# Three more turns through DRAM blocks, four bias additions on GpSimd, the inner hat on ScalarE and key loads of half the size

## The chip, the core and the metric

The kernel runs on one core of a Trainium2 chip. The metric is the device time of one execution in microseconds. The kernel before took 3769.52 us, the median of three runs (3765.85 to 3770.04).

The core's engines run side by side, each through its own list of instructions in order: TensorE (PE in the profile, its weight loads PEld), VectorE (DVE), ScalarE (ACT), GpSimd (POOL) and SyncE (SP), which here only issues transfers. An instruction that waits for another engine or a transfer holds up all that stand behind it on its own engine.

## What is computed

Input `x` is four images of 64 x 64 pixels with 256 channels, in float32. First comes full self-attention within each image, then a deformable convolution (DCNv3) and an MLP. Cut to what matters:

```python
q, k, v = x @ wq + bq, x @ wk + bk, x @ wv + bv          # per image, 4096 pixels
x = gamma * (softmax(q @ k.T) @ v) + x

h = ln(x, ln1_g, ln1_b)
x_proj = h @ inproj_w + inproj_b
x1 = depthwise_conv_3x3(h, dw_w) + dw_b
x1 = gelu(ln(x1, dwln_g, dwln_b))
offset = x1 @ off_w + off_b                               # 16 groups x 9 points x (x, y)
mask = softmax(x1 @ mask_w + mask_b)                      # over the 9 points
out = sum over points of mask * bilinear(x_proj, point + offset)
x = x + out @ outproj_w + outproj_b
h = ln(x, ln2_g, ln2_b)
x = x + gelu(h @ fc1_w + fc1_b) @ fc2_w + fc2_b
```

## The kernel before, in words

**Tiling.** 256 pixels (4 image rows) are a unit; there are 64 units, 16 an image. A unit goes through these stages, each a Python function that returns named steps:

- `project` (from line 1391): load the unit's pixels, turn them so that channels lie on partitions, make keys, queries and values. `value_bias` (line 1453) adds the value bias on VectorE while it moves the values out of PSUM. For the first image the values go straight to the tiles `V`, for the others to DRAM (`vd`), from where `value_load` brings them.
- `Attention` (line 1474): works on two units of queries at once. Keys come from DRAM in four loads `k0` to `k3` of 512 KB into two buffers, issued on SP. Step `e<j>` multiplies keys by queries (PE, line 1544), `x<j>` takes exponentials (ACT, line 1554), `wa<j>` and `wb<j>` multiply them with the values (PE, line 1565). `own` loads the pixels for the residual.
- `front` (line 1585): `inverse` and `residual` divide by the softmax sum and add the residual, `stats`, `shift` and `norm` make the first layer norm, `turn` transposes its result on PE (four 128 x 128 transposes through `transposed`, line 347), `scale` applies gain and bias, `image` copies into the convolution's input `hs`, `project_in` is `inproj_w` and `store` adds its bias and sends it to DRAM (`xp`). `keep` adds the output projection's bias to the residual and sends that to DRAM (`x1d`).
- `plan` (line 1644): nine taps of the depthwise convolution on VectorE into `cv` (line 1670), `turn` back to pixels on partitions (PE, line 1683), a layer norm, `turn2` (PE, line 347), `gelu`, the offset and mask heads, and then the bilinear weights as products of three hats an axis: `hat0` and `hat2` are relu(-d) and relu(d) on ScalarE (line 1734), `hat1` is 1 - hat0 - hat2 on VectorE (line 1738).
- `sample` (line 1869): loads windows of `xp` (`win`), and multiplies and adds them with the weights on VectorE (lines 1880 and 1888, 1280 elements a partition each).
- `back`, by `finish` (line 1948): output projection, residual, layer norm, MLP. `raised` (line 1989) adds the last bias on VectorE.

**Turning through DRAM blocks.** VectorE's transpose instruction turns 32 x 32 blocks inside a tile and does not move blocks between partitions. So the kernel has a second way to turn: the tile is written to DRAM (`ways`), read back by four transfers that put the 32 x 32 blocks in their mirrored places (`in_blocks`, line 70, through `blocks`, line 285), and one VectorE instruction then turns all blocks (`swapped`, line 290). Before, this serves `project` of the images after the first (directly from the input) and the two turns of `back` (line 1955 and 1991) for all but the first pair of row groups and the last six. A turn on PE needs no transfer.

**Statistics.** Each layer norm has two small GpSimd instructions on 128 x 2 elements (lines 304 and 305) between VectorE's `stats` and `shift`. Apart from a few setup instructions that is all that GpSimd computes.

**Order.** The order on PE, VectorE, ScalarE and GpSimd is written out by hand in tables: `WHEN` (line 355) gives each step of each stage a place in a slot of nominally 120, and `LATE` holds other places for the first and last slots. Steps of about six stages of different units are so interleaved in each slot. The places are only sorted; they are no times. A slot holds two units.

The kernel also contains a general version of the whole pass for inputs whose values leave a safe range. It is in the program, but isn't executed with these inputs.

Of the kernel before, what the change touches and what calls it, by code (L numbers as in the profile page):

```python
# [8 lines left out]
F32 = mybir.dt.float32  # L9
# [11 lines left out]
def tile_attention_dcnv3_block(  # L21
# [26 lines left out]
    P = 128  # L48
# [234 lines left out]
    ways = dram.tile([2, 256, C], F32, name="ways")  # L283

    def blocks(name, src, t0=0):
        t = p1.tile([P, C // P, 256], F32, tag="xs", name=f"bl_{name}")
        in_blocks(t, src, t0, 2)
        return t

# [32 lines left out]
    def scaled(pt, g, b, name, m=256, hT=None):  # L322

        if hT is None:
            hT = p3.tile([P, C // P, 256], F32, tag="cT", name=f"hT_{name}")
# [16 lines left out]
    def transposed(src, name, n=2, pool=None, tag="m"):  # L342

        pt = (pool or ps).tile([P, C // P, 256], F32, tag=tag, name=f"pt_{name}")
        for k in range(C // P):
            for i in range(n):
# [11 lines left out]
            "value_bias": 7.4,  # L358
# [3 lines left out]
            "value_bias": 7.4,  # L362
        },
        "projecta": {
            "load": 0.5607, "copy": 16.2617, "turn": 19.72, "keys": 32.3364, "key_bias": 36.8224,
            "values": 63.7383, "value_bias": 68.2243,
        },
        "projectb": {
            "load": 65.9813, "turn": 79.72, "copy": 80.9346, "keys": 136.6355, "key_bias": 137.757,
            "values": 167.6636, "value_bias": 171.4019,  # L370
        },
        "tablesa": {
            "gelu0": -44.2991, "gelu1": -13.6449, "exp": -12.8972,
        },
        "tablesb": {
            "gelu0": -9.1589, "gelu1": 54.0187, "exp": 61.1215,
        },
        "fronta": {
            "inverse": -7.6636, "residual": -6.9159, "stats": -6.1682, "shift": -3.5514, "norm": 19.2523,
            "turn": 22.243, "scale": 24.486, "image": 24.8598, "project_in": 25.9813, "store": 33.4579,  # L380
            "keep": 40.1869,
        },
        "frontb": {
            "inverse": 4.2991, "residual": 10.6542, "stats": 20.0, "shift": 49.5327, "norm": 52.1495,
            "turn": 60.3738, "scale": 65.6075, "image": 66.3551, "keep": 71.215, "project_in": 78.3178,
            "store": 84.6729,
        },
        "plana": {
            "tap0": 25.6075, "tap1": 26.729, "tap2": 28.5981, "tap3": 30.4673, "tap4": 31.215, "tap5": 32.7103,
            "tap6": 34.2056, "tap7": 34.5794, "tap8": 38.6916, "turn": 40.9346, "stats": 45.0467,  # L390
            "shift": 48.0374, "norm": 49.1589, "turn2": 51.028, "gelu": 51.7757, "heads0": 54.7664,
            "heads1": 55.514, "bias0": 57.0093, "bias1": 61.8692, "mask_exp": 62.243, "sums": 62.9907,
            "carry": 63.3645, "invert": 64.8598, "weigh": 66.729, "hat0": 69.7196, "hat2": 70.8411,
            "hat1": 75.3271, "nearer": 78.6916, "near": 79.0654, "mask": 81.3084, "product0": 81.6822,
            "y_copies0": 83.1776, "y0": 83.5514, "product1": 84.2991, "y1": 85.7944, "y_copies1": 88.0374,
            "x_copies": 88.785, "x": 92.8972, "count": 111.5888, "bounds": 246.9159,
        },
        "planb": {
            "tap0": 69.3458, "tap1": 73.8318, "tap2": 80.5607, "tap3": 86.1682, "tap4": 89.1589,
            "tap5": 89.9065, "tap6": 91.028, "tap7": 93.6449, "tap8": 94.7664, "turn": 96.6355,  # L400
            "carry": 98.5047, "stats": 99.6262, "shift": 102.6168, "norm": 104.8598, "turn2": 107.8505,
            "gelu": 108.5981, "heads0": 113.4579, "heads1": 114.5794, "bias0": 116.0748, "bias1": 116.8224,
            "hat0": 117.9439, "mask_exp": 118.6916, "sums": 119.4393, "hat2": 122.4299, "hat1": 122.8037,
# [104 lines left out]
    }  # L508


    LATE = {
        "summinga": {
            32: {
                "rows01": -68.11728, "rows02": -65.41895, "rows03": -60.32211, "rows04": -52.22712,
# [1842 lines left out]
```

## Time and profile before

| what | value | where it is from |
|---|---|---|
| median of 3 runs | 3769.52 us (3765.85 to 3770.04) | times |
| profiled execution | 3769.71 us | times |
| its span, first to last instruction | 3767.9 us | profile |
| PE busy, weight loads (PEld) busy | 3674.0 us (98%), 3089.0 us (82%) | profile, part 1 |
| DVE busy | 3494.9 us (93%) | profile, part 1 |
| ACT busy | 2286.7 us (61%) | profile, part 1 |
| POOL busy | 464.4 us (12%) | profile, part 1 |
| granted TensorE clock | 0.993 mean | profile, cores |
| transfers | 507.21 MB, 135 GB/s mean | profile, part 3 |

The span is the time from the first to the last instruction that the profiler saw. Engine shares are of that span. In groups of instructions (part 5 of the profile) a line reads: source line, engine, operation, written tile <- read tiles, shape, count, then busy time in us, mean ns of one, and the idle time of the engine just before them with what ended it. In the timeline a row reads: start in us, duration in us, engine, line, operation.

### The profile page before, as it was taken

The page shows a single profiled execution, that of the slowest core. Times are in us where ns is not written, and L with a number is a line of the kernel's source. Part 1 is how long each engine was busy: PE and PEld are TensorE (multiplying, and loading weights), DVE is VectorE, ACT ScalarE, POOL GpSimd, SP SyncE. Part 2 cuts the span into 40 slices and gives each one's busy share as a digit, 9 for nine tenths or more (in the row PEclk, how much of TensorE's full clock was granted, in tenths as well). Part 3 has the DMA queues.
Part 4 walks back from the last instruction along what each step waited for, and adds up shares of the span by engine and source line. Part 5 has one row for each costly group of instructions (what it writes and reads, how often), then busy time and mean ns, then how long its engine had stood idle before and what let it go on. Part 6 is the DMA issues. An engine that isn't in the chain of part 4 may idle for free.

```text
span 3767.9 us, 49959 instructions
## 1 busy us (share of the span) xinstructions
PE 3674.0 (98%) x16770; PEld 3089.0 (82%) x16770; DVE 3494.9 (93%) x6107; ACT 2286.7 (61%) x4164; POOL 464.4 (12%) x444
## 2 busy tenths in 40 slices
PE   7999999999999999999999999999999999999978
PEld 5888888888888888888888888888888888887757
DVE  2289999999999999999999999999999999999996
ACT  2465666665666665666665666665666666666633
POOL 1001011101111101111101101101101110110021
PEclk9999999999999999999999999999999999999989
DMA  6354455555555454546555545545645444444331
GB/s 170 105 150 130 132 140 137 138 149 155 135 152 147 134 133 131 142 129 173 145 137 147 144 126 139 139 131 153 160 121 150 130 121 114 129 132 133 109 90 53
DMA packets 609404, 507.21 MB, mean 135 GB/s; under 512 B 380816, under 2 KB 538576, under 8 KB 609136
## 3 DMA queue, kind: packets, MB, share of 16 engines
q1 hardware_dynamic: 599232, 497.00, 49.6%
q10 hardware_dynamic: 8320, 3.43, 0.4%
q0 software_dynamic: 1584, 3.47, 0.3%
q8 instruction: 135, 2.21, 0.3%
q14 instruction: 133, 1.09, 0.1%
HBM read 351.31 MB, written 152.44 MB: 134 GB/s over the span
## 4 chain that ended last, share of the span: by engine, by line
DVE 62%; PE 18%; issue 7%; DMA 4%; POOL 4%; ACT 3%; SPq 1%; DVEq 0%; ACTq 0%; POOLq 0%
DVE pw L1888 14%; DVE pw L1880 13%; DVE cv L1670 8%; PE acc L1565 8%; DVE pr L1793 3%; PE pmlp L2024 2%; PE ph L2007 2%; POOL rstd_b L305 2%; DVE pw L1893 1%; DVE om L1716 1%; DVE hat L1785 1%; PE e L1544 1%; POOL rstd_b L304 1%; DVE st_b L300 1%; DVE x L1595 1%
## 5 line engine op out<-in xcount | busy, mean ns | idle before, releaser
L1565 PE MATMUL acc<-V,ex 128*128 128x257 f32 x8192 | 1888.2, 380 | 1.3 <-ACT ex L1554 1.2
L1565 PEld LDWEIGHTS acc<-V,ex 128*128 128x128 f32 x8192 | 1546.7, 190 | 239.8 <-issue 20.7
L1880 DVE TENSOR_TENSOR pw<-win,wn 128x1280 f32<-128x1280 f32 x640 | 944.7, 1482 | 10.7 <-DMA win<-xp 1.7
L1888 DVE TENSOR_TENSOR pw<-pw,pw 128x1280 f32<-128x1280 f32 x492 | 727.8, 1479 | 0.4
L1554 ACT ACTIVATE ex<-e 128x512 f32<-128x512 f32 x1024 | 553.3, 590 | 260.0 <-PE e L1544 229.9
L2007 PE MATMUL ph<-hT_b,f1w 128*128 128x256 f32 (+1 forms) x2080 | 509.0, 382 | 23.3 <-ACT gT L2015 13.6
L2007 PEld LDWEIGHTS ph<-hT_b,f1w 128*128 128x128 f32 x2080 | 386.9, 192 | 100.1 <-ACT gT L2015 30.0
L2024 PE MATMUL pmlp<-f2w,gT 128*128 128x256 f32 x2048 | 463.2, 380 | 0.3 <-ACT gT L2015 0.3
L1670 DVE SCALAR_TENSOR_TENSOR cv<-hs,dw,cv 128x256 f32<-128x256 f32 (+1 forms) x1076 | 433.9, 462 | 3.9 <-ACT cv L1666 3.8
L2024 PEld LDWEIGHTS pmlp<-f2w,gT 128*128 128x128 f32 x2048 | 386.3, 191 | 53.4 <-ACT gT L2015 0.7
L1544 PE MATMUL e<-qs,kT 128*128 128x512 f32 (+1 forms) x1056 | 418.3, 479 | 10.1 <-issue 6.2
L2015 ACT ACTIVATE gT<-ph,f1b 128x256 f32<-128x256 f32 (+1 forms) x520 | 237.7, 468 | 191.9 <-PE ph L2007 189.6
L1554 ACT ACT_TABLE_LOAD x220 | 282.3, 1283 | 8.3 <-PE acc L1565 4.8
L304 POOL TENSOR_SCALAR rstd_b<-mv_b 128x2 f32<-128x2 f32 (+1 forms) x65 | 59.8, 920 | 1658.4 <-DVE mv_b L302 1596.6
L1544 PEld LDWEIGHTS e<-qs,kT 128*128 128x128 f32 x1056 | 196.3, 191 | 42.8 <-ACT ex L1554 9.3
L318 ACT ACTIVATE xn_b<-x1b,nm_b,rstd_b 128x256 f32<-128x256 f32 x128 | 70.0, 593 | 238.1 <-DVE nm_b L310 237.3
L1707 PE MATMUL po<-om_w,ge 128*128 128x432 f32 x512 | 201.7, 535 | 4.4 <-ACT ge L1700 3.6
L1793 DVE TENSOR_TENSOR pr<-hat 128x1296 f32<-128x1296 f32 x128 | 192.6, 1505 | 5.8 <-ACT us L1808 1.8
L318 ACT ACTIVATE xn_p<-pc,nm_p,rstd_p 128x256 f32<-128x256 f32 x128 | 65.3, 559 | 218.0 <-DVE nm_p L310 218.0
L2015 ACT ACT_TABLE_LOAD x136 | 174.5, 1283 | 2.4
L1707 PEld LDWEIGHTS po<-om_w,ge 128*128 128x128 f32 x512 | 98.0, 193 | 74.9 <-issue 51.7
L304 POOL TENSOR_SCALAR rstd_f<-mv_f 128x2 f32<-128x2 f32 x64 | 25.1, 393 | 1078.9 <-DVE mv_f L302 1029.3
(224 smaller groups left out, 4042.8 us busy)
## 6 DMA issues: line engine op xcount, KB each, us to landing
win<-xp SPq DMA_DIRECT2D x536, 320.0 KB, 4.4
kT<-kd SPq DMA_DIRECT2D x132, 512.0 KB, 3.9
omd<-om SPq DMA_DIRECT2D x63, 432.0 KB, 2.5
x<-in_x_dram SPq DMA_DIRECT2D x64, 256.0 KB, 3.2
x1d<-x SPq DMA_DIRECT2D x64, 256.0 KB, 2.8
xp<-xq SPq DMA_DIRECT2D x128, 128.0 KB, 2.4
x1b<-x1d SPq DMA_DIRECT2D x63, 256.0 KB, 3.0
spd<-sp SPq DMA_DIRECT2D x63, 256.0 KB, 2.2
```

The costliest lines, as they stand in the source:

```text
L318: nc.scalar.activation(xn[:, i, :], s, AF.Identity, bias=nm[:, i : i + 1], scale=st["r"][:, i : i + 1])
L1544: nc.tensor.matmul(e, lhsT=self.kT[t // 8][:, t % 8, :], rhs=q, start=True, stop=not self.general)
L1554: nc.scalar.activation(ex, self.es[r], AF.Exp)
L1565: nc.tensor.matmul(self.acc[u][:, i, :], lhsT=ex[:, i * P : (i + 1) * P], rhs=V[j][:, jj, :], start=(t == 0), stop=(t == NT - 1),)
L1670: nc.vector.scalar_tensor_tensor(dst, src, dw[:, k, j : j + 1], dst, ALU.mult, ALU.add)
L1707: nc.tensor.matmul(st["po", i], lhsT=st["ge"][:, k, i * P : (i + 1) * P], rhs=om_w[:, k, :], start=(k == 0), stop=(k == 1),)
L1793: nc.vector.tensor_mul(pr.rearrange("p a b c d g -> p a b (c d g)"), hat[:, :, i, 1, :].unsqueeze(1).to_broadcast([P, 3, 3, S]), hat[:, :, ...
L1880: nc.vector.tensor_mul(st[i, r].rearrange("p d (g c) -> p (d g) c", c=GC), src.rearrange("p d (g c) -> p (d g) c", c=GC), wns[v][:, i, r] ...
L1888: nc.vector.tensor_add(st[i, 0], st[i, 0], st[i, r])
L2007: nc.tensor.matmul(ph[:, :m], lhsT=f1w[:, k, c * P : (c + 1) * P], rhs=st["hT"][:, k, :m], start=(k == 0), stop=(k == 1),)
L2015: nc.scalar.activation(st["gT"][:, c, :m], st["ph", c][:, :m], AF.Gelu, bias=f1b[:, c : c + 1])
L2024: nc.tensor.matmul(po, lhsT=st["gT"][:, c, i * P : (i + 1) * P], rhs=f2w[:, c, :], start=(c == 0), stop=(c == NH - 1),)
```

## The change

Five things are changed, and both order tables are written anew.

1. **Turns.** `front.turn` (layer-normed image), `plan.turn` (convolution) and `plan.turn2` (its normalised form) go through DRAM blocks like the turns of `back`: `sent` writes the tile to one of eight buffers `ways`, `blocks` reads it, `swapped` turns it on VectorE. This holds for units 0 to 57 in `front` and pairs 1 to 57 in `plan`; the rest keep PE. For `back` the range shrinks from pairs 1 to 58 to pairs 1 to 55. Writes of normalised tiles are issued on ScalarE's queue, that of the convolution on SP.
2. **Bias additions.** `keep`, `store` (now a ScalarE copy out of PSUM, then a new step `add`), `raised` and the value bias become GpSimd additions of 128 x 512 elements. The value bias is no longer added to the values: since softmax weights sum to one it is added once to the residual's pixels (new steps `biasa`, `biasb`), and values leave PSUM by a ScalarE copy (`value_copy`).
3. **Inner hat.** `hat1` becomes two ScalarE instructions: |d|, then 1 - |d|.
4. **Keys.** Eight loads of 256 KB instead of four of 512 KB, still into two buffers (each half as large), issued on ScalarE's queue instead of SP's.
5. **Buffers.** `cT` gets four buffers instead of three, `xs` two instead of one.

```diff
-    ways = dram.tile([2, 256, C], F32, name="ways")
+    ways = dram.tile([8, 256, C], F32, name="ways")

     def blocks(name, src, t0=0):
-        t = p1.tile([P, C // P, 256], F32, tag="xs", name=f"bl_{name}")
+        t = p1.tile([P, C // P, 256], F32, tag="xs", bufs=2, name=f"bl_{name}")
         in_blocks(t, src, t0, 2)
         return t
+
+    def sent(k, u, src, engine):
+        way = ways[2 * k + u % 2]
+        engine.dma_start(way.rearrange("(q p) c -> p q c", p=P), src)
+        return way
...
-        def value_bias():
-            bias = bv_s.unsqueeze(1).to_broadcast([P, 2, C])
+        def value_copy():
             if first:
-                nc.vector.tensor_add(V[u][:, :, :C], st["pv"], bias)
+                nc.scalar.copy(V[u][:, :, :C], st["pv"])
             else:
                 vs = p1.tile([P, 2, C], F32, tag="xq", name=f"vs_{n}")
-                nc.vector.tensor_add(vs, st["pv"], bias)
+                nc.scalar.copy(vs, st["pv"])
                 nc.sync.dma_start(vd[u], vs)
...
+        def constant(self, u):
+            nc.gpsimd.tensor_tensor(self.x[u], self.x[u], bv_s.unsqueeze(1).to_broadcast([P, 2, C]), ALU.add)
+
         def keys(self, g):
-            kT = kv.tile([P, 8, P], F32, tag="kT", bufs=2, name=f"kT_{self.n}_{g}")
-            src = kd[self.b].rearrange("r h c n -> (r h c) n")[:, 8 * P * g : 8 * P * (g + 1)]
-            nc.sync.dma_start(kT.rearrange("p t k -> p (t k)"), src)
+            kT = kv.tile([P, 4, P], F32, tag="kT", bufs=2, name=f"kT_{self.n}_{g}")
+            src = kd[self.b].rearrange("r h c n -> (r h c) n")[:, 4 * P * g : 4 * P * (g + 1)]
+            nc.scalar.dma_start(kT.rearrange("p t k -> p (t k)"), src)
...
+        through = b * NU + u < UN - 6 and not general
+
         def norm():
             normalised(st, [att.x[u][:, i, :] for i in range(2)], f"f{n}")
+            if through:
+                st["way"] = sent(1, u, st["xn"], nc.scalar)

         def turn():
-            st["pt"] = transposed(st["xn"], f"f_{n}")
+            if through:
+                st["bl"] = blocks(f"f_{n}", st["way"])
+            else:
+                st["pt"] = transposed(st["xn"], f"f_{n}")
+
+        def swap():
+            st["hT"] = swapped(p3.tile([P, C // P, 256], F32, tag="cT", bufs=4, name=f"hT_f{n}"), st["bl"])
...
         def keep():
-            nc.vector.tensor_add(att.x[u], att.x[u], ob.unsqueeze(1).to_broadcast([P, 2, C]))
+            nc.gpsimd.tensor_tensor(att.x[u], att.x[u], ob.unsqueeze(1).to_broadcast([P, 2, C]), ALU.add)
...
         def store():
-            xq = p1.tile([P, 2, C], F32, tag="xq", name=f"xq_{n}")
-            nc.vector.tensor_add(xq, st["pp"], inb.unsqueeze(1).to_broadcast([P, 2, C]))
+            st["xq"] = p1.tile([P, 2, C], F32, tag="xq", name=f"xq_{n}")
+            nc.scalar.copy(st["xq"], st["pp"])
+
+        def add():
+            xq = st["xq"]
+            nc.gpsimd.tensor_tensor(xq, xq, inb.unsqueeze(1).to_broadcast([P, 2, C]), ALU.add)
...
+        through = 0 < v < UN - 6 and not general
+
+        def send():
+            st["way"] = sent(2, v, st["cv"], nc.sync)
+
         def turn():
+            if through:
+                st["bl"] = blocks(f"c_{n}", st["way"])
+                return
...
+        def swap():
+            st["pc"] = swapped(p3.tile([P, 2, C], F32, tag="cT", bufs=4, name=f"pc_{n}"), st["bl"])
...
+            if through:
+                st["way2"] = sent(3, v, st["xn"], nc.scalar)

         def turn2():
-            st["pt"] = transposed(st["xn"], f"p_{n}", nt)
+            if through:
+                st["bl"] = blocks(f"p_{n}", st["way2"])
+            else:
+                st["pt"] = transposed(st["xn"], f"p_{n}", nt)
+
+        def swap2():
+            st["ge"] = swapped(p3.tile([P, C // P, 256], F32, tag="cT", bufs=4, name=f"ge_{n}"), st["bl"])
...
         def inner_hat():
             hat = st["hat"]
-            nc.vector.scalar_tensor_tensor(
-                hat[:, 1], hat[:, 0], 1.0, hat[:, 2], ALU.subtract, ALU.subtract, reverse0=True
-            )
+            xy = st["om"][:, :nt, : 2 * S].rearrange("p i (t s) -> p i t s", t=2)
+            nc.scalar.activation(hat[:, 1], xy, AF.Abs)
+            nc.scalar.activation(hat[:, 1], hat[:, 1], AF.Identity, bias=every[:, 0:1], scale=-1.0)
...
             if way is not None:
-                st["way"] = ways[(way + 1) // 2 % 2]
-                nc.sync.dma_start(st["way"].rearrange("(q p) c -> p q c", p=P), st["xn"])
+                st["way"] = sent(0, (way + 1) // 2, st["xn"], nc.scalar)

         def raised():
             x1n = st["x1"][:, :n, :]
-            nc.vector.tensor_add(x1n, x1n, f2b.unsqueeze(1).to_broadcast([P, n, C]))
+            nc.gpsimd.tensor_tensor(x1n, x1n, f2b.unsqueeze(1).to_broadcast([P, n, C]), ALU.add)
...
-            way=g0 if 0 < v < UN - 5 and not general else None,
+            way=g0 if 0 < v < UN - 8 and not general else None,
```

`WHEN` and `LATE` get places for the new steps, and all other steps are placed anew. In the steady slots, for example, the two exponent-table steps, the loads of `project` and the steps of `front` stand elsewhere relative to the attention steps.

## The prediction

> **What bounds the kernel now.** First the totals and the slices, then the steady part alone, then the chain, then one stretch in order of time.
>
> ```profile
> PE 3674.0 (98%) x16770; PEld 3089.0 (82%) x16770; DVE 3494.9 (93%) x6107; ACT 2286.7 (61%) x4164; POOL 464.4 (12%) x444
> ...
> PE   7999999999999999999999999999999999999978
> ...
> DVE  2289999999999999999999999999999999999996
> ```
>
> ```profile
> 240.00:3480.00 3240.00, 3214.34 (x14712) 2711.54 (x14710) 3156.11 (x5397) 2053.31 (x3711) 398.03 (x350) 1.00 0.52 138
> ```
>
> That row is one stretch of 3240 us: PE busy 3214 (99%), PEld, DVE 3156 (97.4%), ACT 2053 (63%), POOL 398, granted clock 1.00, transfers 0.52 of their engines' time. Two engines are full at once. VectorE has 84 us of idle time in the stretch, PE 26. The Trainium skill ("Trainium Kernel Development and Optimization", Performance Expectations) warns that busy matmul time flatters PE; so I look at its rate: in the timeline below two value-product matmuls of 257 columns follow each other every 0.22 us (16 in 3.63 us), as everywhere else in the stretch, so PE is really at its pace and sets it. VectorE follows at 2.6% distance.
>
> ```profile
> DVE 62%; PE 18%; issue 7%; DMA 4%; POOL 4%; ACT 3%; SPq 1%; DVEq 0%; ACTq 0%; POOLq 0%
> ```
>
> The chain that ended last runs mostly over VectorE: in the last stretch, 3480 to 3768, VectorE is busy 246.4 of 288 us, PE 246.5. So a gain on PE counts only as far as VectorE can follow, and a loss on VectorE counts almost whole.
>
> ```profile
> 1487.78 1.46 DVE L1888 TENSOR_TENSOR pw<-pw,pw 128x1280 f32<-128x1280 f32 x1
> 1488.02 1.29 POOL L304 TENSOR_SCALAR rstd_p<-mv_p 128x2 f32<-128x2 f32 x1 [4.17 <-DVE mv_p L302]
> ...
> 1488.50 3.63 PE L1565 MATMUL acc<-V,ex 128*128 128x257 f32 x16
> 1489.27 1.49 DVE L1880 TENSOR_TENSOR pw<-win,wn 128x1280 f32<-128x1280 f32 x1
> 1489.40 1.93 POOL L305 TENSOR_TENSOR rstd_p<-rstd_p,minus_half 128x2 f32<-128x2 f32 x1
> ...
> 1492.63 0.66 PE L347 MATMUL pt_p<-ident,xn_p 128*128 128x128 f32 x4
> 1492.91 0.69 DVE L1459 TENSOR_TENSOR vs<-pv,bv_s 128x512 f32<-128x512 f32 x1
> ...
> 1493.13 1.25 PE L1565 MATMUL acc<-V,ex 128*128 128x257 f32 x5
> 1493.51 1.48 DVE L1888 TENSOR_TENSOR pw<-pw,pw 128x1280 f32<-128x1280 f32 x1
> ```
>
> Three things are to be seen. A turn on PE (four transposes) holds PE from 1492.63 to 1493.13: 0.50 us; one of the convolution (1482.41 to 1482.84) 0.43. Successive VectorE instructions overlap by some 0.08 us (1492.91 + 0.69 against 1493.51), so one costs its mean less 0.08. And the GpSimd instruction at 1488.02, which takes 0.22 us elsewhere (at 1461.80), lasts until 0.07 us after the end of VectorE's addition (1489.24), and the next VectorE instruction starts 0.03 us after that end instead of 0.08 before it. The two engines exclude each other: GpSimd waits for VectorE, then VectorE gives up about 0.11 us to a read of two elements a partition.
>
> **The change, part by part.** Rows from the groups by form:
>
> ```profile
> L1630 DVE TENSOR_TENSOR xq<-pp,inb 128x512 f32<-128x512 f32 x64 | 43.7, 684 | 2.1 <-PE pp L1623 2.1
> L1616 DVE TENSOR_TENSOR x<-x,ob 128x512 f32<-128x512 f32 x64 | 43.2, 675 | 0.0
> L1989 DVE TENSOR_TENSOR x1b<-x1b,f2b 128x512 f32<-128x512 f32 x63 | 43.0, 684 | 0.0
> L1459 DVE TENSOR_TENSOR vs<-pv,bv_s 128x512 f32<-128x512 f32 x48 | 32.9, 685 | 4.8 <-DMA vd<-vs 4.8
> L291 DVE STREAM_TRANSPOSE sT<-bl_s 128x512 f32<-128x512 f32 x58 | 40.9, 705 | 0.0
> L1738 DVE SCALAR_TENSOR_TENSOR hat<-hat 128x576 f32<-128x576 f32 x63 | 47.4, 753 | 0.0
> ```
>
> *Turns, PE.* 58 + 57 + 57 turns leave PE, 2 x 3 of `back` return: 166 x 0.43 to 0.50 = 71 to 83 us, taken as 75. On the path, since PE sets the pace.
>
> *Turns, VectorE.* 166 block transposes more at 0.705 - 0.08: +104 us.
>
> *Additions off VectorE.* The four rows, the 16 of the first image (10.6 us) and two half ones: 174 us in 257 instructions, less 257 x 0.08: -154 us. *Inner hat:* 48.2 us in 65: -43 us. Without any further effect VectorE would thus get 154 + 43 - 104 = 93 us lighter.
>
> *Additions on GpSimd.* 257 of 128 x 512 elements with two inputs in SBUF. No row shows one; the nearest are the two small ones above, which show the exclusion but not its length at this size. The rule that speaks against the change is the Trainium skill's "SBUF — State Buffer", Who interferes with whom: a VectorE instruction with two SBUF inputs and a GpSimd instruction that reads SBUF use one shared port, held for the whole instruction, and the later one is fully blocked. Its "GPSIMD Engine Reference", Elementwise, gives 4497 ns for an addition of 2048 elements, so by proportion, an estimate, 1.12 us for 512. By the small rows alone (0.11 us each) the additions would take 28 us from VectorE, and the change would win; by the rule 1.12 + 0.11 = 1.23 us each wherever VectorE has two SBUF inputs. That is most of its time: what has at most one (bias from PSUM 76, statistics 144 + 58, block transposes 116 + 104, reductions 40, additions from PSUM 86 + 56, small ones about 90) is some 770 of 3400 us, 23%. So 0.95 us each, 244 us. The ends are 0.1 (26 us) and 1.25 (321 us). I take 0.95: the small rows show that the lock exists for just this pair of kinds, and a read of 1024 operands through it can't be as short as one of two to four.
>
> *VectorE's sum:* -93 + 244 = +151 us. Of its 84 idle us in the steady stretch I let about half, 45, be used up once PE no longer sets the pace; the rest is small waits and the 0.11 us pieces. +106.
>
> *ScalarE.* 128 copies out of PSUM at 0.585 (row of `xT`): +75; two hat instructions for none, 65 x 2 x 0.674 (row L1734, same shape): +87; table loads fall from 517 to 448 in the new order, 69 x 1.283: -89. Net +73 on 2287, 63 to 65%. It also issues 170 writes of normalised tiles and 264 key loads, some 0.37 us each on its sequencer. A write waits for ScalarE's own activation, so nothing behind it starts for about 0.45 us: at most 77 us, and exponentials stand behind it; eight `ex` buffers and its 35% idle hide that. If they did not, up to 77 us of PE waits.
>
> *Key loads.* On SP they waited 248 us in all for PE; on ScalarE such a wait would hold exponentials back. In the new order each stands behind the last energy step that reads its buffer, and the exponentials behind it need that step anyway: 0, ends -5 and +20.
>
> *SP and transfers.* Block loads grow from 656 to 1320 issues at 0.65 us: SP's issue time goes from 1222 to about 1600 us of 3768, with the loads of windows queued behind. Bytes grow by 166 x 512 KB = 87 MB on 507, transfers from 0.50 to about 0.6 busy. A block load lands in 2.5 us, and the write before it too, so a turn takes some 8 us instead of one; `plan` gets two of these, hidden by the six stages in flight. Cost 0; if the cover fails VectorE waits, ends 0 and +40.
>
> *GpSimd's queue.* POOL goes from 464 to about 1000 us of the span, so it has room. But a small `rstd` instruction can stand behind an addition, and VectorE's `shift` waits for it. Taken as 0, end +60.
>
> **Sum.** 3767.9 + 106 = 3874; the profiled execution (3769.7) and the median (3769.5) are the same within 0.2 us: 3875 us.
>
> **Rivals.** A measurement of this kernel tells some 0.2%, 7.5 us, from no change.
>
> 1. *VectorE becomes the bound through the shared port (forecast).* For: the waits of the small instructions end with VectorE's and VectorE's idle time is nearly gone. Against: it needs the full length at 512 elements. With 0.75 to 1.2 us each: 3820 to 3940. Chance 0.60.
> 2. *The additions are cheap for VectorE (other side).* GpSimd reads in short bursts, or stands mostly beside one-input work. VectorE then falls with PE and PE's 75 us are won: 3695. The point from which it decides: with 0.54 us each, -93 + 257 x 0.54 = +45, just the idle time, and the change is zero; below 0.25 us PE keeps the pace. For: PE is full and loses real work. Against: the row at 1488.02. Chance 0.22, 3690 to 3762.
> 3. *A slower pace through queues on top.* GpSimd's order delays `shift` and ScalarE's writes delay exponentials: half of the 190 statistics find an addition of 1.2 us in front, 114 us on top of the forecast: 3990. For: three additions can stand in a row in the new GpSimd order. Against: the steps are placed anew with room. Chance 0.14.
> 4. *Gains and losses cancel,* or the edit does less than it says. The order of the program as built has 664 fewer transposes on PE, so it does act. 3762 to 3777, chance 0.04.
>
> **Numbers.** Likeliest 3875, its own range 3820 to 3940. The range takes in most of rival 2: 3705 to 3950. Slower 0.60 + 0.14 = 0.74, same 0.04, faster 0.22.
>
> **What would show it.** Right: the 128 x 512 additions on POOL last 1.2 to 2.7 us, VectorE's following instruction starts about a microsecond after the one before has ended, PE shows waits and falls below 97%, and the time per slot of two units rises from 112.3 us (start of one `inverse` to that two units later) to 115 to 117. VectorE's busy time alone would fall, to about 3390, though it is the bound. Wrong: PE still busy to 99% and VectorE's gaps short, or an end of VectorE's waits on `rstd` or on transfers that outweighs the gaps without a releaser.

## The result, and the profile after

The changed kernel takes 4040.62 us (median of 4 runs, 4035.53 to 4041.61), the kernel before 3769.78 us beside it: ratio 1.072 (95% interval 1.070 to 1.0737), so it is 271 us slower. The prediction had the direction and the first cause, but named 3875 us and a range up to 3950. The profiled execution's span is 4033.7 us.

The totals, the slices and the chain of waits of the changed kernel, and then its steady stretch alone (length, then busy us of PE, PEld, DVE, ACT and POOL, granted clock, share of the transfer engines, GB/s):

```profile
PE 3707.1 (92%) x16106; PEld 3038.4 (75%) x16106; DVE 3553.2 (88%) x5950; ACT 2363.3 (59%) x4356; POOL 768.4 (19%) x702
...
PE   6999999999999999999999999998999999989978
...
DVE  1289999998998999998998999998899999999996
...
DVE 19%; PE 5%; DMA 4%; issue 2%; SPq 2%; POOL 1%; ACT 1%; DVEq 0%; ACTq 0%; POOLq 0%
```

```profile
240.00:3480.00 3240.00, 3020.69 (x13052) 2476.45 (x13051) 2988.84 (x4931) 1967.69 (x3611) 612.47 (x541) 0.98 0.64 156
```

No engine is full any more. In the 3240 us PE stands idle for 219 us (before 26) and VectorE for 251 (before 84). A slot of two units takes 120.0 us (median, start of one `inverse` to the one two units later) instead of 112.3. The chain covers only the last third of the span (it breaks off at a transfer, so its shares add up to 33%), but block loads and SyncE's queue are now part of it.

Two things are new. First the additions on GpSimd, in the groups by form:

```profile
L1524 POOL TENSOR_TENSOR x<-x,bv_s 128x512 f32<-128x512 f32 x64 | 117.9, 1843 | 118.3 <-DMA x<-in_x_dram 118.3
L2057 POOL TENSOR_TENSOR x1b<-x1b,f2b 128x512 f32<-128x512 f32 x63 | 109.3, 1736 | 226.8 <-ACT xn_b L323 226.7
L1656 POOL TENSOR_TENSOR x<-x,ob 128x512 f32<-128x512 f32 x64 | 96.8, 1514 | 74.5 <-ACT xn_f L323 74.5
```

and what they do to VectorE, in the timeline (start, duration, engine):

```profile
1700.35 1.27 POOL L1674 TENSOR_TENSOR xq<-xq,inb 128x512 f32<-128x512 f32 x1 [19.28 <-ACT xq L1670]
1700.99 0.71 DVE L296 STREAM_TRANSPOSE pc<-bl_c 128x512 f32<-128x512 f32 x1 [0.76 <-DMA bl_c<-ways]
...
1701.58 1.27 POOL L1656 TENSOR_TENSOR x<-x,ob 128x512 f32<-128x512 f32 x1
1701.62 2.58 DVE L1860 TENSOR_TENSOR pr<-hat 128x1296 f32<-128x1296 f32 x1
...
1702.80 2.54 POOL L1524 TENSOR_TENSOR x<-x,bv_s 128x512 f32<-128x512 f32 x1
...
1704.24 1.27 DVE L1877 TENSOR_TENSOR us<-pr 128x144 f32<-128x144 f32 x1
```

An addition alone takes 1.27 us. The block transpose beside the first one, with one input, keeps its 0.71 us, as the rule that the prediction quoted has it. The product `pr` (1.49 us at 1697.74) takes 2.58: it stands until the second addition has ended. The third addition then stands for `pr`, and the small `us` (0.31 us at 1699.27) takes 1.27 behind the third. So in these rows each addition that meets two-input work costs VectorE about 1.0 us, and it shows inside the durations: summed over all VectorE instructions beside an addition, some 160 us more than the usual (median) length of the same instruction. Without these, VectorE's busy time would be 3553 - 160 = 3393 us.

Second, the block transposes. Before, VectorE had no idle time ahead of them:

```profile
L291 DVE STREAM_TRANSPOSE hT_b<-bl_b 128x512 f32<-128x512 f32 x58 | 40.8, 704 | 0.0
```

In the changed kernel:

```profile
L296 DVE STREAM_TRANSPOSE hT_f<-bl_f 128x512 f32<-128x512 f32 x58 | 40.9, 705 | 10.2 <-DMA bl_f<-ways 9.9 <-issue 0.3
L296 DVE STREAM_TRANSPOSE pc<-bl_c 128x512 f32<-128x512 f32 x57 | 40.3, 708 | 61.0 <-DMA bl_c<-ways 60.2 <-issue 0.8
L296 DVE STREAM_TRANSPOSE ge<-bl_p 128x512 f32<-128x512 f32 x57 | 40.2, 706 | 46.1 <-DMA bl_p<-ways 46.1
L296 DVE STREAM_TRANSPOSE sT<-bl_s 128x512 f32<-128x512 f32 x55 | 38.9, 708 | 49.6 <-DMA bl_s<-spd 49.1 <-issue 0.5
L296 DVE STREAM_TRANSPOSE hT_b<-bl_b 128x512 f32<-128x512 f32 x55 | 38.8, 705 | 53.3 <-DMA bl_b<-ways 39.0 <-DMA out_dram<-x1b 6.7 <-DMA win<-xp 4.8
```

VectorE stands 220 us ahead of these transposes, 204 of them for block loads, and that holds for the old turns of `back` (`sT`, `hT_b`) as for the new ones. The first load is issued 3.4 to 5.5 us behind its write (medians by turn; before 2.3 and 2.5).

### The profile page after: what moved, and what is told of

It is laid out like the page before. It is cut to its first block, busy times and chain, and to the rows that moved or that the text cites. A ratio compares the mean times of both kernels' runs of the same rounds, so it can differ in the third digit from the quotient of the medians.

```text
span 4033.7 us, 50430 instructions
## 1 busy us (share of the span) xinstructions
PE 3707.1 (92%) x16106; PEld 3038.4 (75%) x16106; DVE 3553.2 (88%) x5950; ACT 2363.3 (59%) x4356; POOL 768.4 (19%) x702
## 5 line engine op out<-in xcount | busy, mean ns | idle before, releaser
L1593 PEld LDWEIGHTS acc<-V,ex 128*128 128x128 f32 x8192 | 1571.6, 193 | 318.0 <-issue 41.9
L1957 DVE TENSOR_TENSOR pw<-pw,pw 128x1280 f32<-128x1280 f32 x492 | 741.9, 1508 | 2.0
L2075 PE MATMUL ph<-hT_b,f1w 128*128 128x256 f32 (+1 forms) x2080 | 524.7, 387 | 99.9 <-ACT gT L2083 67.2
L1715 DVE SCALAR_TENSOR_TENSOR cv<-hs,dw,cv 128x256 f32<-128x256 f32 (+1 forms) x1076 | 475.7, 495 | 6.7 <-ACT cv L1711 6.6
L1572 PE MATMUL e<-qs,kT 128*128 128x512 f32 (+1 forms) x1056 | 439.3, 491 | 15.4 <-ACT ex L1582 12.6
L1582 ACT ACT_TABLE_LOAD x189 | 242.5, 1283 | 31.9 <-ACT xn_b L323 11.4
L309 POOL TENSOR_SCALAR rstd_b<-mv_b 128x2 f32<-128x2 f32 (+1 forms) x65 | 26.8, 413 | 1056.9 <-DVE mv_b L307 1044.8
L1674 POOL TENSOR_TENSOR xq<-xq,inb 128x512 f32<-128x512 f32 x64 | 86.4, 1349 | 543.4 <-ACT xq L1670 464.2
L1874 ACT COPY us<-pr 128x144 f32<-128x144 f32 x128 | 39.8, 311 | 230.5 <-DVE pr L1860 230.5
L309 POOL TENSOR_SCALAR rstd_p<-mv_p 128x2 f32<-128x2 f32 (+1 forms) x65 | 59.0, 908 | 583.4 <-DVE mv_p L307 583.4
```

Of the source, the lines that this page charges most:

```text
L1572: nc.tensor.matmul(e, lhsT=self.kT[t // 4][:, t % 4, :], rhs=q, start=True, stop=not self.general)
L1582: nc.scalar.activation(ex, self.es[r], AF.Exp)
L1593: nc.tensor.matmul(self.acc[u][:, i, :], lhsT=ex[:, i * P : (i + 1) * P], rhs=V[j][:, jj, :], start=(t == 0), stop=(t == NT - 1),)
L1674: nc.gpsimd.tensor_tensor(xq, xq, inb.unsqueeze(1).to_broadcast([P, 2, C]), ALU.add)
L1715: nc.vector.scalar_tensor_tensor(dst, src, dw[:, k, j : j + 1], dst, ALU.mult, ALU.add)
L1957: nc.vector.tensor_add(st[i, 0], st[i, 0], st[i, r])
```

## The experiments

Edits are to the changed kernel unless the kernel before is named. All times are medians; the kernel before took 3768.4 to 3770.6 beside them.

### The two suspects, one by one

**No additions.**

```diff
-            nc.gpsimd.tensor_tensor(att.x[u], att.x[u], ob..., ALU.add)
+            pass
```
The three other additions go the same way.

> The changed kernel with the four additions left out (all four biases are left out). Theory P: the whole price of the additions goes, 200 to 300 us, 3740 to 3840. Theory B: nothing waits for the additions, 4000 to 4035. If both count, the gain is 200 to 250 and the idle time of VectorE before its block transposes (220 us in the changed kernel) stays about as it is.

3878.8 us (ratio 1.0284, 1.0267 to 1.0302). The additions are worth 162 us, 0.63 each, less than the 200 to 250 given for the case that both count, and a loss of 109 us stays without any of them. VectorE is busy for 3393.0 us now, just what is left above without the longer durations. The idle time ahead of the block transposes stays too: pc 54.8, hT_b 49.8, ge 47.4, sT 33.7 us. The chain, which covers this kernel whole:

```profile
DVE 56%; DMA 15%; PE 9%; issue 7%; SPq 6%; POOL 3%; ACT 2%; DVEq 0%; ACTq 0%; POOLq 0%
```

Transfers and SyncE's queue are 21% of it, against 5% before. That points to the second cause.

**The additions back on VectorE, in the same places.**

```diff
-            nc.gpsimd.tensor_tensor(att.x[u], ...)
+            nc.vector.tensor_tensor(att.x[u], ...)
```

> The changed kernel with its four additions of 128 x 512 issued on VectorE instead of GpSimd, in the same places. Theory P (shared port): in the changed kernel's trace the 255 additions stretch VectorE's instructions by 162 us beside them and leave gaps; VectorE loses that (200 to 250 us) and takes 154 us of additions back, so 3935 to 4000. Theory B (block loads land late, and the additions cost VectorE nothing): VectorE only gets 154 us heavier, 4150 to 4200.

4033.2 us (ratio 1.0696): between the two ranges, and no slower than with them on GpSimd. The four groups have means of 679 to 687 ns there. Moving an addition of this size to GpSimd saved VectorE nothing.

**The port alone.** The kernel before, with an addition more beside each of its own:

```diff
             nc.vector.tensor_add(att.x[u], att.x[u], ob.unsqueeze(1).to_broadcast([P, 2, C]))
+            nc.gpsimd.tensor_tensor(extra, bv_s..., bv_s..., ALU.add)
```

> The kernel before, with one more GpSimd addition of 128 x 512 beside each of the four VectorE bias additions (257 in all; they read a constant and write a tile that nobody reads, so they are work added, nothing is waited for). It prices the port with the order and the transfers left as they were. If an addition holds VectorE 0.95 us as the prediction has it, 257 x 0.95 = 244 us come on VectorE, less the 66 us that it stood idle in the middle of the kernel before: 3770 + 180 = 3950 (3900 to 4010). If it costs what its neighbours in the changed kernel lost (162 us stretched and about as much idle ahead of the next), the same 3930 to 4010. If GpSimd works beside VectorE with no lock that matters: 3765 to 3800.

3946.5 us (ratio 1.0469, 1.0453 to 1.0485): +177 us where 180 was worked out from 0.95 us each less the idle time. The lock is there, but the two parts of that sum didn't come. Its steady stretch:

```profile
240.00:3480.00 3240.00, 3103.23 (x14011) 2572.09 (x14010) 3160.29 (x5138) 1946.94 (x3531) 727.47 (x544) 1.00 0.50 132
```

VectorE is as busy as before (3156) with 5% fewer instructions in the stretch; the lock sits inside the durations. Its idle time there is 80 us, against 84 before: hardly any of it was used up. And over the whole execution its busy time grew from 3494.9 to 3678.9 us, 0.72 an addition and not 0.95. That 244 - 66 and 184 - 6 are the same is chance. (The extra tile is in bfloat16, and such an addition alone takes 1.03 us, so it is not quite the one of the change.)

**No loads for the three new turns.** Their transposes read a tile that stands still; writes, places and additions stay. Left out is the way back from DRAM.

```diff
-                st["bl"] = blocks(f"f_{n}", st["way"])
+                pass
...
-            st["hT"] = swapped(..., st["bl"])
+            st["hT"] = swapped(..., inw)
```

> The changed kernel without the block loads of the three new turns (front, both of the plan), whose transposes read a tile that stands still: the transposes, their places, the writes and the additions stay, the way back from DRAM is left out with its 12 x 53 DMAs and its latency. Theory D, the round trip of the new turns holds up the engines that wait for them in turn: TensorE's waits fall from 305 us to under 150 and the kernel takes 3880 to 3950 (the additions' port, 160 us, remains). If the round trip costs nothing as the prediction has it: 4000 to 4045.

> As a15_turns_without_loads and the four bias additions left out. What is left of the change is less work on TensorE (75 us) and on VectorE (104 - 154 - 43 = -93 us), and a new order. If the port and the round trip are all that the change costs: 3690 to 3780, at or under the kernel before. If the written order as such is worse: 3800 to 3880, near the 3879 of the kernel without additions.

With additions 3939.2 us, without 3743.6. The four kernels make a table:

| | with block loads | without | price of the loads |
|---|---|---|---|
| with additions | 4040.6 | 3939.2 | 101 |
| without | 3878.8 | 3743.6 | 135 |
| price of the additions | 162 | 196 | |

All else in the change (less work on PE, the hat, the keys, the new order) gains 26 us on the kernel before. The two causes are thus shown by taking each away; 34 us are lost already with either of them alone. The steady stretch of the kernel without both:

```profile
240.00:3480.00 3240.00, 3179.20 (x14187) 2665.27 (x14186) 3103.98 (x5350) 2144.40 (x3923) 282.64 (x351) 1.00 0.58 152
```

Over the whole execution PE is busy 66 us less than in the kernel before (3607.5) and VectorE 109 us less (3385.9), but both stand idle longer in the stretch, 61 and 136 us.

### What about the loads costs

Theories, as the texts name them: the transposes stand too close behind their loads (A), SyncE's queue is loaded (B), two block buffers are too few (C), the length of the way itself (D). Later, E: a late transpose is paid through ScalarE.

**Transposes that don't wait, loads that don't wait.** In one kernel the three new transposes read a still tile but the loads are made; in the other the transposes wait for loads that read the input `x` instead of the written tile.

```diff
-            st["hT"] = swapped(..., st["bl"])
+            st["hT"] = swapped(..., inw)
```
```diff
-                st["bl"] = blocks(f"f_{n}", st["way"])
+                st["bl"] = blocks(f"f_{n}", xs_)
```

> The changed kernel whose three new block transposes read a weight tile that lies still, while the writes and block loads are still made: the values of image, convolution and its normalised form are others. Theory B: the idle time before these three (10 + 61 + 46 us) goes, and what it delays with it: 3880 to 3935. Theory P alone: 4015 to 4040, since the waits only lie where VectorE would otherwise wait for GpSimd.

> The changed kernel whose block loads of the three new turns read the input instead of the tile just written (other values), so that they wait for no write to land, but keep their place in SP's queue. If the round trip (write landing, then loads) makes VectorE wait, nearly as much as without the block wait: 3890 to 3950. If SP's queue holds the loads back, whatever they wait for: 4000 to 4035.

4112.2 and 4030.6 us: the first is 72 us slower, outside both of its ranges, the second gains 10, in the range of SyncE's queue. So the wait for the write to land is worth little. In the first, VectorE's waits moved to an old turn, and PE waits for the addition to `x1b` that comes after that turn and frees its place in PSUM:

```profile
DVE sT L296 <- DMA bl_s<-spd: 184.1, 41, 8.9
...
PE po L1774 <- DVE x1b L2048: 131.3, 26, 9.7
```

(us in total, times, longest.) Before this edit the first row had 47.8 us.

**Later transposes.** Four of the five placed 1 to 10 us later on VectorE:

```diff
+        for i, mine, user in moved:
+            over = [t for t in taken if t > mine + 1e-9]
+            until = min(user, over[1] if len(over) > 1 else user) - 0.02
```

> The changed kernel with four of the five block transposes of a unit (front, first of plan, both of back) placed later in VectorE's written order, by 1 to 10 us: up to just ahead of the step that uses the result or of the next-but-one block load, whichever is first, in slots 2 to 28. Nothing is left out. Theory A, the transposes stand too close behind their loads in the written order (idle before them 61.0 + 53.3 + 49.6 + 10.2 = 174 us in the changed kernel, 0 in the kernel before): these rows fall under 60 us together and the kernel takes 3880 to 3960 us. Theory B, the loads come late because SyncE's queue is full and waits in order; the transposes then wait at the new place nearly as long, or their users do: 4010 to 4060 us, with the idle rows over 120 us or moved to PE.

4120.2 us, slower by 80. The four rows all but vanished, as A has it, but the time didn't follow: `ge`, left in its place, now waits 103.7 us, and PE waits 136.2 us for the later `sT`. A falls as a remedy; the time is above B's range too.

**Stores off SyncE's queue.**

```diff
-            nc.sync.dma_start(x1d_[b * NU + u], att.x[u])
+            nc.gpsimd.dma_start(x1d_[b * NU + u], att.x[u])
```

> The changed kernel with the three stores that follow the GpSimd additions of the front (x1d after keep, two of xp after add) issued from GpSimd's own queue instead of SyncE's: 3 x 64 DMAs leave SyncE's queue, and with them its waits for GpSimd (179.9 + about 80 us of standing at the head). Nothing is left out. Theory B, SyncE's queue holds the block loads back: first load after write falls from 3.7-5.7 us towards the 2.3-2.5 us of the kernel before and the kernel gains 60 to 150 us (3890 to 3980). Theory A, the written order alone: within 25 us of the changed kernel (4015 to 4065). A third way: the stores' descriptors are made by GpSimd under the same port, and it becomes slower: over 4065.

4071.7 us, slower by 31. SyncE's own waits say why fewer issues didn't free it: a load now waits for the later store.

```profile
SPq L1520 <- DMA x1d<-x: 291.8, 46, 13.9
```

It was 8.9 us in 5 waits with the stores on SyncE. The time is in the range of the third way, but its reason isn't seen: those of VectorE's instructions that run beside such an issue, and beside no addition, take no longer than elsewhere (1 us less in all, for 205 of them).

**A third buffer, alone and with all five transposes later.**

```diff
-        t = p1.tile([P, C // P, 256], F32, tag="xs", bufs=2, name=f"bl_{name}")
+        t = p1.tile([P, C // P, 256], F32, tag="xs", bufs=3, name=f"bl_{name}")
...
-    f2b = bcast(fc2_b, C, "f2b")
+    inb = f2b = ob
```

> The changed kernel with three instead of two buffers for the block loads and the key images (12 uses of them in a slot); the room comes from the biases of the inner projection and of the last layer, which are read from the outer projection's tile, so that their values are left out while every addition stays. Theory C, the two buffers hold the loads back: the load behind a write starts earlier (first load 3.7-5.7 us behind the write falls towards 2.5), the idle time ahead of the block transposes (220 us) falls by half or more, and the kernel takes 3900 to 3970 us. Theory A, the written order stands too close to the round trip itself: the loads land no earlier, 4010 to 4050 us.

> The same third buffer, and all five block transposes of a unit placed later in VectorE's written order (each up to its user, or to the third block load after its own), in slots 2 to 28. Theory C, which also has the later transposes of the two-buffer kernel slow because they kept the two buffers (4120 us, with the second transpose of the plan waiting 104 us): with the third one the idle rows fall under 60 us and the kernel gains on both, 3880 to 3960 us. Theory D, a round trip's length itself is on the chain from VectorE through DRAM to TensorE and back, wherever the transpose stands: VectorE's idle rows fall but TensorE's waits grow by as much, 4000 to 4120 us.

4005.8 and 4036.8 us. The buffer is worth some 35 us, not the 70 to 140 that C asked for. With room as well, VectorE's waits for blocks fall to 14 us in the stretch, and PE's grow (`sT` 108.6, `ge` 43.7): that is D's picture.

**Fewer and larger pieces.** One load of whole rows instead of four of 128-byte pieces (the block arrangement is left out), and the same in four parts.

```diff
-        in_blocks(t, src, t0, 2)
+        nc.sync.dma_start(t, src.rearrange("(q p) c -> p q c", p=P))
```

> The changed kernel in which each of the three new turns loads its tile back with one DMA of whole rows (256 KB in 1 KB pieces) in place of four of 64 KB in 128-byte pieces: the same bytes, the same wait for the write and the same wait of the transpose, but 3 DMAs fewer on SyncE's queue per turn (516 of 688) and 256 packets instead of 2048. The arrangement in blocks is left out, so the transposes turn rows that are not blocks. Theory B, the number of DMAs or packets on SyncE's queue is the price: near the kernel without these loads, 3939 to 3965. Theory D, the wait for write and load in turn is the price: 4000 to 4040.

> As a18_one_plain_load, but in four DMAs of 32 rows of partitions each: as many DMAs as the changed kernel, 64 KB each, with 1 KB pieces. Theory B by DMAs (their issue on SyncE, 0.65 us each): as slow as the changed kernel, 4010 to 4045. Theory B by packets: like a18. Theory D: both stay at 4000 to 4040.

4066.3 and 4075.9 us, 26 and 35 more than the changed kernel. But these two times hold work that the changed kernel doesn't have. With the blocks out of place, more sampling points fall too far out, and a repair for such points (`far_round`, of which every kernel here runs one round beside the main pass) runs two rounds more, behind everything else. The last regular store of the changed kernel (SPq: issued by SyncE):

```profile
4022.32 0.34 SPq L2128 DMA_DIRECT2D out_dram<-x1b  x1
```

and of the first of these two, with the start of both rounds:

```profile
3945.76 0.34 SPq L2133 DMA_DIRECT2D out_dram<-x1b  x1
...
3956.12 0.23 DVE L2183 SCALAR_TENSOR_TENSOR f_u_f<-cnt,rev 128x65 f32<-128x65 f32 x1 [1.07 <-issue]
...
4006.48 0.23 DVE L2183 SCALAR_TENSOR_TENSOR f_u_f<-cnt,rev 128x65 f32<-128x65 f32 x1 [6.63 <-PEq L2394]
```

So the work that all share ends 76 us earlier than in the changed kernel, and 60 us earlier in the second (3962.3), where leaving the loads out gave 93 (3929.2). The steady stretches agree:

```profile
240.00:3480.00 3240.00, 3071.21 (x13345) 2522.27 (x13344) 3103.78 (x5037) 2013.22 (x3693) 641.63 (x550) 0.99 0.61 159
```
```profile
240.00:3480.00 3240.00, 3055.49 (x13312) 2512.44 (x13310) 3076.36 (x5024) 2008.71 (x3683) 630.82 (x549) 0.99 0.61 158
```

| | loads in 128-byte pieces | whole rows, four DMAs | whole rows, one DMA | no loads |
|---|---|---|---|---|
| last regular store, us | 4022.3 | 3962.3 | 3945.8 | 3929.2 |
| slot, us | 120.0 | 117.7 | 117.5 | 117.1 |
| VectorE idle ahead of the five block transposes, us | 220 | 127 | 92 | 74 |
| SyncE's time in issues in the stretch, us | 1460 | 1314 | 1096 | 1026 |

From the last store to the end it takes 113.4 us in both, against 11.4 in the changed kernel. Less these 102 us, as an estimate, they would take 3964 and 3974 us: about the range of B, and not that of D. The second has as many DMAs as the changed kernel, so most of the gain comes with the size of the pieces and not with the number of DMAs.

**No reader and a third buffer.** Both edits from above at once.

> The changed kernel in which the three new transposes of a unit read a tile that stands still (their block loads are still made, nobody reads them), as in a5_no_block_wait (4112 us), and with the third buffer of a11_third_buffer (4006 us). It tells which part of the loads is the 101 us that a15 gained. Theory C, the loads are paid through the two buffers that they share with the old turns: with the third one and no reader, 3930 to 3970. If the loads are paid through SyncE's place in the order, where the old turns' loads queue behind them: 4010 to 4120.

4095.8 us, in the range of SyncE's order: it isn't the buffers that the loads hold either, and `sT` waits 183.9 us as in the kernel with two.

What is shown: with the loads in SyncE's queue it takes 101 to 135 us more. Whichever of the waits for the write, the waits of the reader or the shared buffers is lifted, at most some 35 us come back, and the wait turns up at another block load or at PE. With the same bytes in whole rows, waits and buffers as they were, 60 to 76 of 93 us come back, which points to the 128-byte pieces for most of the price. What is not settled is how the pieces cost it, by their longer issue on SyncE (0.63 us for one load of pieces, 0.42 for one of the four of whole rows) or by the transfers themselves (busy 0.64 of the time against 0.61). Nor is the order excluded: SyncE's isn't written in the tables but planned from the program, so these edits also rearrange it. Of SyncE's 2215 other transfers, 93% have the same next one as in the changed kernel where the transposes don't wait, 88% where the loads read `x`, 79 and 74% with whole rows in four DMAs and in one, 70% where the loads are gone. A run with that order held fixed was not made.

### One turn alone, in the kernel before

The front's turn through blocks in 50 units, with and without the hat on ScalarE; then with its chain earlier in the second unit; then in the first unit of a slot only (25 turns). All of them also have the load and copy of the key projection earlier, to free the one block buffer, and the normalisation and turn of `front` at other places.

```diff
+            if through:
+                st["way"] = fways[u % 2]
+                nc.sync.dma_start(st["way"].rearrange("(q p) c -> p q c", p=P), st["xn"])
...
-            "stats": 20.0, "shift": 49.5327, "norm": 52.1495, "turn": 57.6, "swap": 65.4,
+            "stats": 20.0, "shift": 44.5, "norm": 47.1, "turn": 52.6, "swap": 61.4,
```

> The kernel before with two parts of the change only: the inner hat on ScalarE (VectorE -43 us) and the turn of the front's normalised image through DRAM blocks in 50 units, its transpose placed 12 us behind the block load and 15 us behind the write (TensorE -50 x 0.45 = -22 us, VectorE +50 x 0.625 = +31 us). The bias additions stay on VectorE. Theory A, room in the written order makes a block turn as cheap as its instructions: 3735 to 3765. Theory B, four more block loads per unit on SyncE's queue hold others up wherever the transpose stands: 3780 to 3830.

> The kernel before with the front's image turned through DRAM blocks in 50 units and nothing else (the inner hat back on VectorE, where it was; in the run with both, VectorE waited 104.5 us in 25 places for ScalarE's hat and 20 us for a block transpose). TensorE -50 x 0.45 = -22 us, VectorE +31 us, which has 66 us idle. Theory A: 3745 to 3775, and the hat was what cost 145 us. Theory B, four more block loads per unit on SyncE's queue hold the kernel up by themselves: 3800 to 3900.

> The kernel before with the front's turn through DRAM blocks, as in the run c2_front_alone (3864.6 us), and for every second unit the shift, normalisation, block load and transpose placed 4 to 5 us earlier in the written order. In that run one transpose of each slot ended behind ScalarE's place for its reader: ScalarE waited 3.75 us in 25 places (93.7 us), and TensorE 2.5 + 0.9 us in the same slots (72 us for exponentials). Theory E, a late transpose is paid through ScalarE, whose queue TensorE then waits for: both rows fall under 25 us and the kernel takes 3750 to 3790. Theory B, the loads themselves load SyncE's queue: the time stays at 3845 to 3875.

> As c2_front_alone, but only the first unit of each slot goes through DRAM blocks (25 turns), where the transpose stood ready 2.9 us ahead of its reader; the second unit turns on TensorE as before. Theory E: nothing is late, 3755 to 3780. Theory B: half of the 95 us that c2_front_alone lost, about 3817 (3800 to 3835).

3913.1, 3864.6, 3948.2 and 3851.9 us: all slower. Only the second came in one of its ranges, that of B. Each has at least one new wait a slot, of 3 to 5 us, and each another one (the first has that of the second as well). From the waits of the four kernels in this sequence (us in total, times, longest):

```profile
DVE am L1756 <- ACT hat L1752: 104.5, 25, 4.6
```
```profile
ACT hT_f L328 <- DVE hT_f L292: 93.7, 25, 3.8
...
PE e L1545 <- ACT ex L1555: 71.7, 32, 2.9
```
```profile
DVE hT_f L292 <- DMA bl_f<-fways: 113.0, 23, 6.0
```
```profile
PE pt_f L348 <- DVE om L1728: 76.0, 25, 3.5
```

In the second, VectorE waits for none of the new blocks. A transpose that ends 3.75 us behind ScalarE's place for its reader holds ScalarE, PE stands behind the late exponentials, and the slot is longer by 115.0 - 112.3 = 2.7 us, in some 28 slots most of the loss. The third was to cure that and shows no more: the chain moved ahead in the table, but in the second unit its first load came 11.5 us behind the write instead of 5.8, and the wait went to VectorE.

The fourth says little of block turns. Its wait, 76 of the 82 us lost, is at the second unit's turn, which is on PE as before, but stands at 57.6 instead of 60.4 in the table, where the block load stood in the second kernel. No wait for the 25 blocks themselves is in its list. So none of the four prices a block turn by itself, and a run with the moved places and no block turn was not made. No version here beats the kernel before; the 3743.6 us leave out work that is needed.

## Why the prediction failed, point by point

- **"Cost 0; if the cover fails VectorE waits, ends 0 and +40" (the step that failed).** The turns' way through DRAM costs 101 us, or 135 without the additions. "Hidden by the six stages in flight" was argued from the number of stages, not from the room between a load and its transpose: before, the old turns' `sT` came only 2.5 us (median, least 0.2) behind the landing of its blocks. And only the length of a turn, 8 us, was looked at, where the runs point to the loads' 128-byte pieces for most of the price: whole rows, with the same waits, give 60 to 76 us back. How the pieces cost it stays open.
- **"VectorE would thus get 93 us lighter" (failed too).** It did get lighter, by 109 us, and PE by 66, but without loads and additions only 26 us are gained; rival 2, which is this case, had 75. VectorE waits there for the old turns' loads, 35 us for `sT` and 30 for `hT_b`, where before it didn't wait for them.
- **The lock on the port, 0.95 us an addition, and 45 us of idle time used up (the mechanism right, the sum by luck).** The lock is there, and VectorE's busy time without it is the 3390 us that were forecast. But an addition costs 0.63 us (162 us for 257), 0.76 without the loads (196) and 0.69 in the kernel before (177), and in the last, where it could be seen, hardly any idle time is used up. Both errors cancel: 244 - 45 = 199, measured 162 to 196.
- **The sum.** Forecast -93 + 199 + 0 = +106. Measured, in the same terms, -26 + 196 + 101 = +271. Of the 165 us that were missing, 101 are the loads and 67 the gain that didn't come; the additions took 3 less.
- **Rival 3, "a slower pace through queues on top", 3990.** Near in size, wrong in place: it named GpSimd's order ahead of `shift` and ScalarE's writes. VectorE's waits for `rstd` fell from 56 to 39 us; the queue was the one in front of the block loads.
- **The signs.** PE under 97%: 92. The slot 115 to 117 us: 120.0; without the block loads 117.1. Of the signs of being wrong, waits on transfers came: 184 of the 238 us of VectorE's waits in the stretch are for block loads.

## What to carry to other kernels

When every engine runs its list in order and two are full, price an added round trip by the room that its nearest neighbours have between landing and use, and by the size of its pieces, not by the stages in flight. Before moving an elementwise operation to GpSimd, compare its length there with the price on VectorE: with two SBUF inputs on both sides VectorE paid 0.63 to 0.76 us an addition here, as much as doing it itself (0.68). When a wait is removed and the time stays, look for the same microseconds at the next engine before calling the wait harmless. And where an edit changes values, see that the program still does the same work before comparing times: here the total said slower, and the shared work was faster.

## What the hardware showed that was not expected

The granted clock falls behind PE's pauses. Windows of the changed kernel (second figure: PE busy; the third from the end: clock):

```profile
1330.00:1340.00 10.00, 9.17 (x39) 6.84 (x38) 8.16 (x10) 5.89 (x14) 0.00 (x0) 1.00 0.71 192
1340.00:1350.00 10.00, 7.62 (x29) 5.85 (x28) 9.46 (x18) 7.39 (x17) 5.07 (x3) 0.88 0.51 117
1350.00:1360.00 10.00, 10.00 (x45) 8.55 (x44) 10.00 (x19) 5.71 (x10) 1.91 (x3) 0.95 0.66 187
```

Behind a pause of 2.4 us in the second row the clock is 0.88 and 0.95; in the kernel before each of 50 such windows has 1.00. Over the steady stretch it is 0.98. The Trainium skill ("TensorE: Matmul & The Clock Gate", Part 1) has the clock at half rate after a window of some 3.4 us without enough activity. The trace's clock records, of which the rows show the means, agree: here one piece of 3.41 us at half rate, from 1347.62 on. In the steady stretch there are 24 such pieces, of 102 us together, all with their start on one grid of 3.41 us (before: one piece). In the grid window just ahead of each PE stood idle for 1.8 to 3.1 us, and none of this kernel's windows with more than 2.0 us was followed by the full clock. A single long pause isn't needed: ahead of 17 of the 24 none was longer than 3 us.

So a PE that has less to do can also do it more slowly: its busy time rose from 3674 to 3707 us with 664 matmuls fewer, and without loads and additions, where the clock is 1.00, the same matmuls take 3607 us. How much of that is the clock was not separated.
